# Two-layer image attention on one Trainium2 core: softmax sums from a column of ones in v, and layer-norm input transposed in one pass

## The chip, the cores and the metric

The kernel runs on one NeuronCore of a Trainium2 chip. Its time is the device time of one execution in microseconds (us); a result is the median of several executions. Five engines work side by side, each in the order of its own queue: TensorE (PE; its weight loads are shown as PEld), VectorE (DVE), ScalarE (ACT), GpSimd (POOL) and SyncE (SP). They wait for one another by semaphores. DMA queues move data between memories.

## The reference

The input `x` is 4 images of 32x32 positions with 768 channels, float32. Two layers follow, each `x = x + attention(groupnorm(x))`, with 12 heads of 64 channels over all 1024 positions of an image.

```
layer 0: q, k, v = heads(x @ Wq + bq), ...           # no norm on q, k, v
layer 1: q, k, v = layer_norm(dwconv3x3(heads(x @ w_qkv.T + b_qkv)))   # over the 64 channels of a head
attn = softmax(q @ k.T / 8 + rel_h(q)[:, :, :, :, None] + rel_w(q)[:, :, :, None, :])
o    = attn @ v            (layer 1: + q)
out  = o @ Wp + bp
```

`layer_norm` subtracts the mean over the 64 channels of a head and divides by the standard deviation; then it multiplies by `g` and adds `b`, each of 64 values. Before `g` and `b` the 64 channels of a normed vector therefore sum to zero. `rel_h` and `rel_w` are products of q with tables of relative positions.

## The kernel before, in words

**Tiling.** Work goes in pairs of heads, since two heads of 64 channels fill the 128 partitions. There are 8 stages (image, layer), in the order (0,0), (1,0), (0,1), (1,1), (2,0), (3,0), (2,1), (3,1), and 6 pairs in each: 48 pairs, 24 of each layer. Attention of a pair (`attend`) has two chunks of 512 queries. A chunk has two groups of four key tiles of 128. For a group TensorE makes four score tiles `s` (128 keys x 2 heads x 512 queries), ACT takes their exponential into `e` (L760), and later TensorE multiplies `v` with them into `av` (L775). The softmax's denominator comes from DVE: it adds all eight `e` tiles of a chunk into `acc` (L767 once, L769 six times), and TensorE sums `acc` over the keys with a matrix of ones into `z` (L717). ACT and DVE make the inverse from `z` (L724 to L733), and DVE multiplies it onto `weighed`, a copy of `av` (L710).

**Order.** The order on TensorE, DVE, ACT and POOL is written out by hand. `attend` is a generator that stops 8 times in a chunk, so 16 steps in a pair. At each step a table `events` runs pieces of other work: the preparation of the next pair (`plan`: number of the step, piece), group norm of the next stage, projection of the stage before (`project`). What `copy(av)` leaves behind is worked off by `more()`: `sums`, `result` and `finish`, one each time that a group of scores or of `av` has been issued.

**Preparing a pair of layer 1.** For each of q, k and v: products with the weights (`padded`, tile `qkv` of L131), ACT puts them into a padded image (L520), DVE makes the 9 taps of the convolution (`taps`, L535 and L537), and then:

- `centre`: TensorE multiplies the convolved image, as the stationary operand, with a 128x128 matrix `CENTRE` (identity less the mean of each head). That transposes it, tokens on partitions, and takes the mean off at once. The two halves of columns are two matmuls (`halves`, L131). Tile `ln_c`; ACT writes its square into `squared` (L550) and itself into `c` (L551).
- `squares`: DVE sums `squared` over each head (L555). `norm`: ACT and DVE make the inverse root (L153 to L160), and DVE multiplies (L566), for v straight into the attention's operand `vt`.
- `back`: q and k are transposed back by TensorE (L573, tile `ln_t`), and ACT writes them (L488, L489, L497).
- `positions` and `split` make the position bias from q (tile `rel`, L595 to L612); POOL's queue spreads it by DMA into `bias` (L622).

**PSUM.** Of eight banks, two are for a score tile `a`, one for `av`, one is `small`; two places of two banks each (`place_b`, left, and `place_c`, right) hold in turn the second and third score tile of a group and single banks for other work. `bank()` hands the singles out in a fixed rotation, `behind_scores` (b, b, c, c) or `behind_av` (c, c, small, b, b). A score pair in a place waits until both singles there have been read.

**Shared memory.** `shared` is one large SBUF tile in parts: two `centred`, two padded images, two `convolved`, one `squared`.

The functions that the diff touches:

Of the kernel before, what the change touches and what calls it, by code (L numbers as in the profile page):

```python
# [9 lines left out]
F32 = mybir.dt.float32  # L10
F32R = mybir.dt.float32r
I32 = mybir.dt.int32
AF = mybir.ActivationFunctionType
# [21 lines left out]
NSMALL = 81  # L35


IDENT, GROUP, CENTRE, HEADS, ONES = 0, P, 2 * P, 3 * P, 3 * P + 2
NCONST = 3 * P + 2 + D


LIMIT = 1e15
# [3 lines left out]
def two_layers(ctx: ExitStack, tc: tile.TileContext, keep, x_in, wqkv, wproj, rels, windows, vrow, small, const, onehot, picks, out):  # L46
# [78 lines left out]
    def small_bank(name):  # L125
        return ps_small.tile([P, 512], F32, tag="small", name=name)

    def halves(ps, a, b, start=True, stop=True, **kw):

        for lo in (0, D):  # L130
            nc.tensor.matmul(ps[lo : lo + D], a[:, lo : lo + D], b, start=start, stop=stop, **kw)  # L131
# [15 lines left out]
    def col(c, lo=0, hi=P):  # L147
        return sm[lo:hi, c : c + 1]
# [50 lines left out]
    def in_turn(what, of):  # L199
        counts[what] += 1  # L200
        return of[counts[what] % 2]
# [166 lines left out]
    class Pair:  # L368
# [170 lines left out]
        def centre(self, s):  # L539

            y = self.y[s]
            self.c[s] = c = in_turn("c", centred)
            for h in range(2):
                cols = slice(h * HALF, (h + 1) * HALF)
                ps = bank("ln_c")
                first = h * (HALF + S)
                for t in range(NKT // 2):
                    tokens = slice(first + t * P, first + (t + 1) * P)
                    halves(ps[:, t * P : (t + 1) * P], y[:, tokens], cst[:, CENTRE : CENTRE + P])
                nc.scalar.activation(squared[:, cols], ps, AF.Square)  # L550
                nc.scalar.copy(c[:, cols], ps)  # L551

        def squares(self, s):
            self.v = v = stat.tile([P, 2 * NKT], F32, tag="lnv", name="lnv")
# [3 lines left out]
        def norm(self, s):  # L558
            r = rsqrt(self.v, 2 * NKT, "ln")
            c = self.c[s].rearrange("p (a d) -> p a d", d=D)  # L560
            dst = c
            if s == 2:

                self.make_vt()
                dst = self.vt.rearrange("p t (j d) -> p (t j) d", d=D)
            nc.vector.tensor_tensor(dst, c, r.unsqueeze(2).to_broadcast([P, 2 * NKT, D]), ALU.mult)  # L566

        def back(self, s, h):

# [55 lines left out]
        def plan(self):  # L625

            Q, K, V = 0, 1, 2
            if not self.layer and not in_sevens(self.i):
                return [
                    (0, lambda: self.plain(Q, 0)),  # L630
                    (2, lambda: self.plain(Q, 1)),
                    (4, lambda: self.plain(K, 0)),
                    (5, lambda: self.positions(0)),
                    (6, lambda: self.plain(K, 1)),
                    (7, lambda: self.positions(1)),
                    (8, lambda: self.split()),
                    (8, lambda: self.plain_v(0)),
                    (10, lambda: self.plain_v(1)),
                ]
            if not self.layer:  # L640
                pieces = [
                    (0, lambda: self.sevens(Q, False)),
                    (2, lambda: self.sevens(Q, True)),
                    (6, lambda: self.positions(0)),
                    (8, lambda: self.positions(1)),
                    (10, lambda: self.split()),
                ]
                if self.hp % 2 == 0:
                    pieces += [(8, lambda: self.sevens(V, False)), (10, lambda: self.sevens(V, True))]
                return [(r + shift(self.i), piece) for r, piece in pieces]  # L650

            pieces = [
                (-8, lambda: self.padded(Q, 0)),
                (-6, lambda: self.padded(Q, 1)),
                (-4, lambda: self.padded(K, 0)),
                (-2, lambda: self.padded(K, 1)),
                (2, lambda: self.padded(V, 0)),
                (4, lambda: self.padded(V, 1)),
                (3, lambda: self.centre(Q)),
                (5, lambda: self.squares(Q)),  # L660
                (7, lambda: self.norm(Q)),
                (8, lambda: self.centre(K)),
                (9, lambda: self.back(Q, 0)),
                (9, lambda: self.back(Q, 1)),
                (10, lambda: self.squares(K)),
                (10, lambda: self.positions(0)),
                (11, lambda: self.positions(1)),
                (12, lambda: self.norm(K)),
                (12, lambda: self.split()),
                (13, lambda: self.centre(V)),  # L670
                (14, lambda: self.back(K, 0)),
                (14, lambda: self.back(K, 1)),
                (14, lambda: self.squares(V)),
                (15, lambda: self.norm(V)),
            ]

            taps = (
                (Q, -4, (2, 2, 2, 2, 1)),
                (K, 2, (2, 2, 2, 2, 1)),
                (V, 8, (2, 2, 3, 2)),  # L680
            )
            for s, r, counts in taps:
                lo = 0
                for n in counts:
                    pieces.append((r, lambda s=s, lo=lo, n=n: self.taps(s, lo, lo + n)))
                    r, lo = r + 1, lo + n
            return pieces
# [4 lines left out]
    def attend(pair, os):  # L692
# [12 lines left out]
        for c in range(T // QC):  # L705
            cols = slice(c * QC, (c + 1) * QC)

            def copy(av):
                weighed = one.tile([P, QC], F32, tag="weighed", name="weighed")
                nc.scalar.copy(weighed, av)  # L710
                return weighed

            def sums(weighed, acc, c=c):

                z = small_bank("z")
                for j in range(2):
                    nc.tensor.matmul(  # L717
                        z[j * D : (j + 1) * D, :], cst[:, ONES : ONES + D], acc[:, j, :],
                        start=True, stop=True,
                    )  # L720
                at = 2 * (pair.i * (T // QC) + c)
                t = work.tile([P, QC], F32, tag="t", name="t", bufs=1)
                inv = work.tile([P, QC], F32, tag="inv", name="inv", bufs=1)
                nc.scalar.activation(t, z, AF.Copy, accum_out=seen[:, at : at + 1])  # L724

                nc.scalar.activation(inv, t, AF.Ln, bias=tiny)
                nc.scalar.activation(inv, inv, AF.Exp, scale=-1.0, accum_out=seen[:, at + 1 : at + 2])
                return weighed, t, inv
# [12 lines left out]

            def finish(inv, cols=cols):

                if not pair.layer:
                    nc.scalar.activation(q[:, cols], inv, AF.Identity, bias=col(pair.column(2)))

            for g in range(0, NKT, 4):
                es = []
# [14 lines left out]
                more()  # L763
                if g == 0:
                    av = ps_av.tile([P, QC], F32, tag="av", name="av")
                    acc = work.tile([P, 2, QC], F32, tag="acc", name="acc", bufs=1)
                    nc.vector.tensor_tensor(acc, es[0], es[1], ALU.add)  # L767
                for e in es[2 * (g == 0) :]:
                    nc.vector.tensor_tensor(acc, acc, e, ALU.add)  # L769
                yield  # L770
                yield
                for t, e in enumerate(es):
# [6 lines left out]
                other_work(behind_av)  # L779
                more()  # L780
                if g + 4 == NKT:
                    rest.extend((sums, result, finish))
                    found = (copy(av), acc)
                yield
                yield

# [148 lines left out]
    for k, stage in enumerate(stages):  # L935
        call, sums, products = project(stage, oss[k])
        first = (k + 1) * NC * n_steps
        if k + 1 == len(stages):
            at(first - 12, call)
            for r, *what in ((-12, range(5), (0,)), (-10, range(5), (1,)), (-6, (0,), (2,))):  # L940
                at(first + r, lambda sums=sums, what=what: sums(*what))
            continue
        at(first + 2, call)
        late = stages[k + 1][1]
        for r, what in ((1, (0,)), (6, (1,)), (8, (2,)), (9, (3,)), (10, (4,))) if late else ((4, (0, 1)), (5, (2,)), (6, (3, 4))):
            at(first + r, lambda sums=sums, what=what: sums(what))

        for r, n in zip((9, 11, 13, 15, 17, 19) if late else (7, 9, 11, 13, 14, 15), (2, 1) * 3):
            for _ in range(n):
                at(first + r, lambda products=products: next(products))  # L950
# [259 lines left out]
def _laid_out(inp):  # L1210
# [24 lines left out]
    const[:, CENTRE : CENTRE + P] = eye - head  # L1235
    const[:, HEADS : HEADS + 2] = np.kron(np.eye(2), np.full((D, 1), 1.0 / D))
    const[:, ONES : ONES + D] = 1.0
    key = np.arange(T)
    onehot = np.concatenate([np.arange(S)[:, None] == key // S, np.arange(S)[:, None] == key % S])

# [36 lines left out]
```

## Time and profile before

| | |
|---|---|
| median of 3 runs | 3901.6 us (3901.35 to 3903.21) |
| the profiled execution | 3898.63 us, its span 3896.8 us |
| mean granted TensorE clock | 0.996 |
| TensorE busy | 3826.2 us (98% of the span) |
| DVE busy | 2674.1 us (69%) |
| ACT busy | 1849.1 us (47%) |
| POOL busy | 412.1 us (11%) |

The page of the profile lists busy time by engine, the span in 40 slices with busy tenths in each, DMA queues, the chain of work that ended last, and groups of instructions. A group's line has: line of the kernel, engine, operation, written and read tiles, shapes, number of instructions; then busy time in us and the mean duration in ns; then the idle time of the engine before them and what ended it. A float32 matmul is two instructions in these counts. Matmuls overlap, so the mean of one is longer than what it adds; the distance from one group's start to the next is what it costs. In a list of waits each line has who waited, for what, the sum in us, how often, and the longest.

### The profile page before, as it was taken

Reading aid. Unit: us, or ns where it says so; the run is one execution under the profiler, and the core shown is the slowest. Engines: PE = TensorE matmul, PEld = TensorE weight load, DVE = VectorE, ACT = ScalarE, POOL = GpSimd, SP = SyncE. Lnnn points to the kernel's source line nnn. Section 1 sums busy time; section 2 is a strip of 40 time slices with the busy share of each in tenths; the row PEclk is TensorE's granted clock in tenths of the full one; section 3 lists DMA queues with packets and bytes.
Section 4 is the critical chain, followed back from the end, with each engine's and each line's share of the span. In section 5 each row is a group of like instructions: output and inputs, shape, how many; then the busy total and the mean of one; then the engine's idle time right before and its main releaser. Section 6 shows DMA issues by size and latency. Waiting matters only on the chain.

```text
span 3896.8 us, 79900 instructions
## 1 busy us (share of the span) xinstructions
PE 3826.2 (98%) x34748; PEld 1720.1 (44%) x34748; DVE 2674.1 (69%) x3088; ACT 1849.1 (47%) x2741; POOL 412.1 (11%) x776
## 2 busy tenths in 40 slices
PE   8999999999999999999899999999999999999998
PEld 3535535544344443444445445355443444434442
DVE  2566454558789987799653554454686898878885
ACT  2455434445255553456434554254553555525562
POOL 0111000110000110000010010011100010000010
PEclk9999999999999999999999999999999999999999
DMA  4344452321421213311144132522124121142123
GB/s 148 105 118 124 124 165 61 106 71 39 119 90 35 51 49 94 115 35 39 44 133 124 51 79 60 176 59 72 43 56 153 35 58 42 39 119 58 35 48 95
DMA packets 184710, 318.11 MB, mean 82 GB/s; under 512 B 24352, under 2 KB 77472, under 8 KB 184352
## 3 DMA queue, kind: packets, MB, share of 16 engines
q1 hardware_dynamic: 122912, 212.19, 17.3%
q0 software_dynamic: 61440, 100.71, 11.3%
q8 instruction: 277, 4.54, 0.5%
q14 instruction: 81, 0.66, 0.1%
HBM read 172.23 MB, written 39.91 MB: 54 GB/s over the span
## 4 chain that ended last, share of the span: by engine, by line
PE 86%; DVE 11%; issue 1%; DMA 1%; ACT 1%; SPq 0%; POOL 0%; DVEq 0%
PE qkv L131 18%; PE s L753 15%; PE av L775 15%; PE m1m L131 4%; PE m3m L131 4%; PE m4m L131 4%; PE s L755 4%; DVE shared L537 3%; PE p3p L131 3%; DVE acc L769 3%; PE p1p L131 3%; PE p4p L131 3%; PE ln_c L131 3%; PE rel L595 3%; PE z L717 2%; PE m L131 2%
## 5 line engine op out<-in xcount | busy, mean ns | idle before, releaser
L760 ACT ACTIVATE e<-s 128x1024 f32<-128x1024 f32 x768 | 776.7, 1024 | 406.2 <-PE s L755 372.8
L769 DVE TENSOR_TENSOR acc<-acc,e 128x1024 f32<-128x1024 f32 x576 | 705.6, 1225 | 182.1 <-ACT e L760 130.4
L753 PE MATMUL s<-q,k 64*128 64x512 f32 x3072 | 816.5, 608 | 4.7 <-ACT e L760 3.8
L131 PE MATMUL qkv<-xn,wqkv_t 128*64 128x512 f32 x3648 | 813.4, 595 | 4.1 <-DVE gmean L324 4.1
L537 DVE SCALAR_TENSOR_TENSOR shared<-shared,sm 128x1056 f32<-128x1056 f32 x576 | 758.6, 1317 | 15.0
L755 PE MATMUL s<-bias,ones 64*128 64x512 f32 x1536 | 615.5, 794 | 4.7 <-DMA bias<-whole 2.5
L775 PE MATMUL av<-e,vt 128*64 128x512 f32 x2624 | 593.9, 594 | 0.0
L622 POOL DMA_DIRECT2D bias<-high x384 | 204.1, 551 | 3225.9 <-ACT high L611 2988.5
L131 PEld LDWEIGHTS qkv<-xn,wqkv_t 128*64 128x64 f32 x3648 | 253.7, 137 | 487.2 <-issue 480.5
L520 ACT ACTIVATE shared<-qkv,sm 128x512 f32<-128x512 f32 (+1 forms) x288 | 129.1, 501 | 633.0 <-PE qkv L131 633.0
L753 PEld LDWEIGHTS s<-q,k 64*128 64x128 f32 x3072 | 283.8, 188 | 260.8 <-issue 214.9
L775 PEld LDWEIGHTS av<-e,vt 128*64 128x64 f32 x2624 | 184.3, 137 | 347.0 <-issue 321.9
L767 DVE TENSOR_TENSOR acc<-e 128x1024 f32<-128x1024 f32 x96 | 117.5, 1224 | 274.0 <-ACT e L760 265.4
L755 PEld LDWEIGHTS s<-bias,ones 64*128 64x128 f32 x1536 | 150.2, 188 | 193.1 <-issue 188.0
L622 POOL DMA_DIRECT2D bias<-whole x384 | 206.9, 567 | 104.3 <-DVE whole L612 96.4
L710 ACT COPY weighed<-av 128x512 f32<-128x512 f32 x96 | 56.3, 586 | 268.8 <-PE av L775 268.8
L131 PEld LDWEIGHTS ln_c<-cst,shared 128*64 128x64 f32 x2304 | 130.4, 137 | 47.5 <-issue 36.0
L595 PEld LDWEIGHTS rel<-q,rel 64*32 64x32 f32 x6144 | 111.9, 106 | 80.7 <-issue 60.6
L131 PE MATMUL ln_c<-cst,shared 128*64 128x128 f32 x2304 | 138.3, 273 | 5.5 <-ACT high L611 2.5
L131 PE MATMUL m4m<-xn,wqkv_t 128*64 128x512 f32 x528 | 122.3, 599 | 4.0 <-issue 3.0
L595 PE MATMUL rel<-q_t,rel 64*32 64x32 f32 x6144 | 123.6, 195 | 2.1 <-issue 2.1
L405 DVE TENSOR_TENSOR shared<-shared,m3m 128x512 f32<-128x512 f32 x66 | 45.4, 687 | 115.8 <-PE m3m L131 115.7
(151 smaller groups left out, 4223.5 us busy)
## 6 DMA issues: line engine op xcount, KB each, us to landing
bias<-high POOLq DMA_DIRECT2D x384, 128.0 KB, 2.8
bias<-whole POOLq DMA_DIRECT2D x384, 128.0 KB, 3.0
wqkv_t<-in_wqkv SPq DMA_DIRECT2D x78, 384.0 KB, 3.1
wqkv_t<-mixed SPq DMA_DIRECT2D x66, 384.0 KB, 3.1
wproj_t<-mixed SPq DMA_DIRECT2D x48, 384.0 KB, 3.3
wqkv_t<-in_wqkv SPq DMA_DIRECT2D x66, 192.0 KB, 2.5
xn<-in_x SPq DMA_DIRECT2D x24, 512.0 KB, 8.4
x<-in_x SPq DMA_DIRECT2D x48, 256.0 KB, 3.3
```

Of the source, the lines that this page charges most:

```text
L131: nc.tensor.matmul(ps[lo : lo + D], a[:, lo : lo + D], b, start=start, stop=stop, **kw)
L520: nc.scalar.activation(self.pad[s][:, rows, there : there + src.shape[2]], src, AF.Identity, bias=col(self.column(s)))
L537: nc.vector.scalar_tensor_tensor(y, window, tap, y, ALU.mult, ALU.add)
L595: nc.tensor.matmul(ps[lo : lo + S, k * S : (k + 1) * S].rearrange("p (b c) -> p b c", b=2), rel[rows, 2 * self.layer + i, first : first + ...
L622: nc.gpsimd.dma_start(sets, some.unsqueeze(1).to_broadcast([D // 2, 2, QC]))
L717: nc.tensor.matmul(z[j * D : (j + 1) * D, :], cst[:, ONES : ONES + D], acc[:, j, :], start=True, stop=True,)
L753: nc.tensor.matmul(ps[:, j, :], k[rows, keys], q[rows, cols], start=True, stop=False)
L755: nc.tensor.matmul(ps[:, j, :], ones[rows, keys], bias[c][rows, kt // 2, :], start=False, stop=True,)
L760: nc.scalar.activation(e, ps, AF.Exp)
L767: nc.vector.tensor_tensor(acc, es[0], es[1], ALU.add)
L769: nc.vector.tensor_tensor(acc, acc, e, ALU.add)
L775: nc.tensor.matmul(av[j * D : (j + 1) * D, :], pair.vt[:, kt, j * D : (j + 1) * D], e[:, j, :], start=(kt == 0), stop=(kt == NKT - 1),)
```

## The change

**Layer 1's denominators.** The last channel of each head's `v` in `vt` is overwritten with ones after the norm (`memset` in `norm`). The last row of each head in `av` is then the sum of its exponentials. `copy` sends that row by two DMAs from ACT's queue to the 64 partitions of the head, tile `t`. `acc` and its adds stay only for layer 0. Since the normed `v` sums to zero over a head, its last channel's result is minus the sum of the others: `sums` multiplies `weighed` with a new 128x128 constant `WHOLE` (identity, last column -1, corner 0) in two halves, into the bank that `z` had, and ACT copies it back into `weighed`. A step `landed`, which issues nothing, is put before `sums`, so `sums` and `result` come one `more()` later each. Before the last stage's projection one piece moves from step -6 to -4.

**The norm's input.** `centre` only transposes (`nc.tensor.transpose` with the identity, one matmul per tile). DVE sums each head's 64 channels from PSUM, and a second DVE operation takes 1/64 of it off while it moves the tile to `c`. The square is one ACT instruction over all 1024 columns from `c`, a piece of its own (`square`), one or two steps later; `squares` moves one step back.

```
-                    halves(ps[:, t * P : (t + 1) * P], y[:, tokens], cst[:, CENTRE : CENTRE + P])
-                nc.scalar.activation(squared[:, cols], ps, AF.Square)
-                nc.scalar.copy(c[:, cols], ps)
+                    nc.tensor.transpose(ps[:, t * P : (t + 1) * P], y[:, tokens], ident)
+                of = sums[:, h * NKT : (h + 1) * NKT]
+                heads = ps.rearrange("p (a d) -> p a d", d=D)
+                nc.vector.tensor_reduce(of, heads, AX.X, ALU.add)
+                nc.vector.scalar_tensor_tensor(
+                    c[:, h * HALF : (h + 1) * HALF].rearrange("p (a d) -> p a d", d=D),
+                    of.unsqueeze(2).to_broadcast([P, NKT, D]), -1.0 / D, heads, ALU.mult, ALU.add,
+                )
+
+        def square(self, s):
+            nc.scalar.activation(squared, self.c[s], AF.Square)
...
             nc.vector.tensor_tensor(dst, c, r.unsqueeze(2).to_broadcast([P, 2 * NKT, D]), ALU.mult)
+            if s == 2:
+                nc.vector.memset(dst[:, :, D - 1 :], 1.0)
...
                 (3, lambda: self.centre(Q)),
-                (5, lambda: self.squares(Q)),
+                (4, lambda: self.square(Q)),
+                (6, lambda: self.squares(Q)),
...
-                (10, lambda: self.squares(K)),
+                (10, lambda: self.square(K)),
+                (11, lambda: self.squares(K)),
...
-                (14, lambda: self.squares(V)),
+                (14, lambda: self.square(V)),
+                (15, lambda: self.squares(V)),
...
             def copy(av):
+
                 weighed = one.tile([P, QC], F32, tag="weighed", name="weighed")
                 nc.scalar.copy(weighed, av)
-                return weighed
...
+                if not pair.layer:
+                    return weighed, acc
+                t = work.tile([P, QC], F32, tag="t", name="t", bufs=1)
+                for rows in heads:
+                    nc.scalar.dma_start(t[rows], weighed[rows.stop - 1 : rows.stop, :].unsqueeze(1).to_broadcast([1, D, QC]))
+                return weighed, t
...
+            def sums(weighed, of, c=c):
+
+                z = small_bank("z" if not pair.layer else "whole")
                 at = 2 * (pair.i * (T // QC) + c)
-                t = work.tile([P, QC], F32, tag="t", name="t", bufs=1)
                 inv = work.tile([P, QC], F32, tag="inv", name="inv", bufs=1)
-                nc.scalar.activation(t, z, AF.Copy, accum_out=seen[:, at : at + 1])
+                if pair.layer:
+                    t = of
+                    halves(z, cst[:, WHOLE : WHOLE + P], weighed)
+                    nc.scalar.copy(weighed, z)
+                    nc.scalar.activation(inv, t, AF.Copy, accum_out=seen[:, at : at + 1])
+                else:
+                    t = work.tile([P, QC], F32, tag="t", name="t", bufs=1)
+                    for j, rows in enumerate(heads):
+                        nc.tensor.matmul(z[rows, :], cst[:, ONES : ONES + D], of[:, j, :], start=True, stop=True)
+                    nc.scalar.activation(t, z, AF.Copy, accum_out=seen[:, at : at + 1])
...
                 if g == 0:
                     av = ps_av.tile([P, QC], F32, tag="av", name="av")
-                    acc = work.tile([P, 2, QC], F32, tag="acc", name="acc", bufs=1)
-                    nc.vector.tensor_tensor(acc, es[0], es[1], ALU.add)
-                for e in es[2 * (g == 0) :]:
-                    nc.vector.tensor_tensor(acc, acc, e, ALU.add)
+                if not pair.layer:
+                    if g == 0:
+                        acc = work.tile([P, 2, QC], F32, tag="acc", name="acc", bufs=1)
+                        nc.vector.tensor_tensor(acc, es[0], es[1], ALU.add)
+                    for e in es[2 * (g == 0) :]:
+                        nc.vector.tensor_tensor(acc, acc, e, ALU.add)
...
-                    rest.extend((sums, result, finish))
-                    found = (copy(av), acc)
+                    rest.extend((landed, sums, result) if pair.layer else (sums, result, finish))
+                    found = copy(av)
...
-            for r, *what in ((-12, range(5), (0,)), (-10, range(5), (1,)), (-6, (0,), (2,))):
+            for r, *what in ((-12, range(5), (0,)), (-10, range(5), (1,)), (-4, (0,), (2,))):
```

More of the change, by code (lines that the diff above doesn't have):

```diff
@@ L35 @@
 NSMALL = 81
-IDENT, GROUP, CENTRE, HEADS, ONES = 0, P, 2 * P, 3 * P, 3 * P + 2
-NCONST = 3 * P + 2 + D
+IDENT, GROUP, CENTRE, HEADS, ONES, WHOLE = 0, P, 2 * P, 3 * P, 3 * P + 2, 3 * P + 2 + D
+NCONST = 4 * P + 2 + D
 LIMIT = 1e15
@@ L542, in centre @@
             self.c[s] = c = in_turn("c", centred)
+            sums = stat.tile([P, 2 * NKT], F32, tag="mean", name="mean")
             for h in range(2):
-                cols = slice(h * HALF, (h + 1) * HALF)
                 ps = bank("ln_c")
@@ L710, in copy, with landed @@
                 nc.scalar.copy(weighed, av)
-                return weighed
[L713 to L720, printed above, removed]
+                if not pair.layer:
[4 more added lines that the diff above has]
+                return weighed, t
+            def landed(*found):
+                return found
+            def sums(weighed, of, c=c):
+                z = small_bank("z" if not pair.layer else "whole")
                 at = 2 * (pair.i * (T // QC) + c)
-                t = work.tile([P, QC], F32, tag="t", name="t", bufs=1)
                 inv = work.tile([P, QC], F32, tag="inv", name="inv", bufs=1)
-                nc.scalar.activation(t, z, AF.Copy, accum_out=seen[:, at : at + 1])
+                if pair.layer:
[8 more added lines that the diff above has]
+                    nc.scalar.activation(t, z, AF.Copy, accum_out=seen[:, at : at + 1])
                 nc.scalar.activation(inv, t, AF.Ln, bias=tiny)
@@ L742, in finish @@
             def finish(inv, cols=cols):
-                if not pair.layer:
-                    nc.scalar.activation(q[:, cols], inv, AF.Identity, bias=col(pair.column(2)))
+                nc.scalar.activation(q[:, cols], inv, AF.Identity, bias=col(pair.column(2)))
             for g in range(0, NKT, 4):
@@ L1237, in _laid_out @@
     const[:, ONES : ONES + D] = 1.0
+    whole = np.eye(D)
+    whole[:, -1] = -1.0
+    whole[-1, -1] = 0.0
+    const[:, WHOLE : WHOLE + P] = np.kron(np.eye(2), whole)
     key = np.arange(T)
```

## The prediction

> **What bounds the kernel now.** I read the page first: busy shares, slices, then the chain that ended last.
>
> ```profile
> PE 3826.2 (98%) x34748; PEld 1720.1 (44%) x34748; DVE 2674.1 (69%) x3088; ACT 1849.1 (47%) x2741; POOL 412.1 (11%) x776
> PE  8999999999999999999899999999999999999998
> DVE  2566454558789987799653554454686898878885
> PE 86%; DVE 11%; issue 1%; DMA 1%; ACT 1%; SPq 0%; POOL 0%; DVEq 0%
> ```
>
> TensorE has work in every slice. A busy row can still hide slack, so I laid its timeline end to end. A run of 24 qkv instructions always takes 5.15 to 5.30 us to the next group's start, an av run 3.43 to 3.58. Everything above the usual spacing adds up to 58 us in 3897. So a microsecond taken out of TensorE's stream is a microsecond of time, and other engines matter only where they make it wait. DVE is the candidate: 8 to 9 tenths in layer 1's slices.
>
> The list of waits, TensorE alone, shows how little that is today:
>
> ```profile
> PE p1p L131 <- DVE os_sums L850: 5.8, 4, 1.4
> PE s L753 <- ACT e L760: 3.8, 3, 1.5
> PE ln_t L573 <- DVE shared L566: 3.4, 2, 1.7
> PE z L717 <- DVE acc L769: 1.8, 1, 1.8
> ```
>
> So taking `acc` off DVE is worth little by itself. The other half touches TensorE: `ln_c`. First the groups, each shape by itself (busy, mean ns), then a stretch of TensorE's timeline (start, us):
>
> ```profile
> L131 PE MATMUL ln_c<-cst,shared 128*64 128x128 f32 x2304 | 138.3, 273 | 5.5 <-ACT high L611 2.5 <-DVE shared L537 2.3 <-DVE t_ln L157 0.7
> L573 PE MATMUL ln_t<-cst,shared 128*128 128x128 f32 x384 | 52.4, 279 | 3.4 <-DVE shared L566 3.4
> ...
> 1009.92 5.37 PE L131 MATMUL qkv<-xn,wqkv_t 128*64 128x512 f32 x24
> 1015.12 1.92 PE L131 MATMUL ln_c<-cst,shared 128*64 128x128 f32 x32
> 1016.87 2.74 PE L131 MATMUL p4p<-os_sums,wproj_t 128*64 128x512 f32 x12
> ...
> 1030.70 1.09 PE L573 MATMUL ln_t<-cst,shared 128*128 128x128 f32 x8
> 1031.72 5.37 PE L131 MATMUL qkv<-xn,wqkv_t 128*64 128x512 f32 x24
> ```
>
> A `centre` call has 8 tiles of 128x128. Today it issues 32 instructions (two column halves, two passes each) and holds TensorE for 1016.87 - 1015.12 = 1.75 us. Two `back` calls transpose 8 tiles of the same size with 8 instructions, 1.02 us. The new `centre` is the second form.
>
> [...] a quarter of the instructions, 1.02 against 1.75 us; the time ratio is 1.7, and I use the time. [...] after holes the granted clock is 0.87 in the stretch 1846 to 1884 us. [...] The nearest row is L845, which reads 512 from PSUM in 0.75 us; I take that for the second operation[...].
>
> **Part by part.**
>
> (1) `centre` on TensorE. 72 calls (24 pairs, three parts), each 1.75 - 1.02 = 0.73 us shorter: 52.6. Followed by scores, ln_c took 1.85 (20 calls): 2.0 more. Entering full-width mode costs 0.10 (qkv to ln_c 5.15, qkv to ln_t 5.25): 7.2 back. **-47.4 us**, all on the path. If the entry costs nothing, -55; if leaving costs 0.10 too, -40.
>
> (2) `centre` off ACT, onto DVE. ACT loses 144 squares and 144 copies (0.60, 0.59) and gets 72 squares of 1024 from SBUF (about 1.05, L611): -97 us. [...] What matters is when the bank comes free: ACT finished 3.15 us after ln_c's start. An idle DVE would finish half one at about 0.8 + 1.45 = 2.25, half two at 3.7. A DVE behind its queue is later, and scores, `back` and products wait for these banks.
>
> (3) Layer 1 without `acc`. 48 chunks lose 7 adds of 1.22: DVE -411. The memset of ones is 24 times about 0.1. DVE's balance is -206 us.
>
> (4) z stays two halves of the same shape (0.91), and moves from after the scores to after av: no change in TensorE time. ACT gets a copy of z (0.59, 48 times) and issues 96 DMAs. None is issued by ACT now; SP's take 0.32 to 0.49 each, so some +35 us, against the 97 freed. Per chunk two issues put 0.7 us ahead of the next exps; the first exp has about 1 us before the third `a`-bank score needs it. Bounds: 0, and 0.5 us a chunk (24) if an issue takes twice that. I take 0. Landing: 128 KB pieces of bias land in 2.8 to 3.0 us; from copy to use lie a scores group and an av, 4.55 + 3.43. Hidden, with 5 us to spare; SP and POOL are not passed.
>
> (5) `result` two steps later, squares one step later. `weighed` is free again before the next av copy (DVE may be some 13 us late). Nothing on the path except at the end, below.
>
> **Where DVE's new duty meets TensorE**, by replaying the queues with the rows' durations. In a usual layer-1 pair:
> - Q's first half sits in the bank pair that the third score needs, 3.3 us after ln_c's start; DVE has caught up by then (no acc, result later), so 2.25: slack 1.
> - K's banks are needed after qkv, about 6.8 us: slack 3.
> - V's second half is needed by `back(K)` after av, at 4.5. Ahead of it DVE has K's norm, the split and two taps: they start when r_ln is there (acc no longer delays them) and end 5.15 us later, some 1.4 us after ln_c's start. Then 2.8: just in time, slack 0.3. I take 0.1 for each of 20: +2.
> - The projection piece three steps into a pair (4 times): two taps and 2.8 us of `centre` go before the L850 add that TensorE waits for; 6.95 us after ln_c's start against 6.1, so 0.85 each: +3.4.
> - Group norm's `gmean` behind V's centre (3 times): +1.8.
>
> Where layer 1 is prepared while layer 0 still runs (2 pairs), acc stays: DVE had some 77 us of work in 79 and gets 8.4 more. Q's squares then come 4 us later, ACT's exps queue behind them (1.8 us), V's banks come late (1.7): +3.8 each, **+7.6**; from 0 to 20.
>
> The two pairs before layer 0 or the end, with no qkv to fill in, are where holes are today:
>
> ```profile
> core 0: us, PE busy (x) PEld busy (x) DVE busy (x) ACT busy (x) POOL busy (x), PEclk, DMA share, GB/s
> ...
> 1846.00:1884.00 38.00, 29.21 (x394) 14.53 (x392) 29.32 (x35) 22.05 (x32) 8.30 (x16) 0.87 0.26 57
> 3757.00:3797.00 40.00, 31.80 (x434) 17.33 (x432) 31.43 (x38) 26.63 (x39) 8.30 (x16) 0.87 0.23 54
> ```
>
> There the chain is DVE: taps, four adds, K's norm, `whole`, then the bias DMA. Without the adds `whole` comes some 6 us earlier, of which 1.5 is already counted in (1): -4.3 each, **-8.6**; from 0 to -14. What is late next is ACT, which must do z's chain (2.9) and the square (1.0) before it empties rel's banks: 2.6 us of waiting stay.
>
> The tail: acc's wait before z goes (1.95), but z now follows the first products, and ACT's chain with one more copy starts later: the x22 products start 13.0 us after av instead of 11.7: +1.3.
>
> Sum: -47.4 - 8.6 + 2 + 3.4 + 1.8 + 7.6 + 1.3 = **-39.9**. The profiled execution took 3898.6 (span 3896.8), 3.0 below the median of the three runs, so: 3858.7 there, **3861** as a median.
>
> **The rivals.**
>
> A, DVE is never late: only (1) and the holes, and the usual DVE-made waits shrink too: -47 to -56, 3846 to 3854. For it: DVE has 206 us less to do. Against: where it is late is decided in two or three places. Chance 0.20.
>
> B, half is given back: V's slack of 0.3 is wrong by one tap (1.31) in 20 pairs, 20 us, or ACT's DMA issues delay exps by 0.5 a chunk: 3880 to 3890. Chance 0.17.
>
> C, slower: DVE becomes the bound through bank release. If it reaches every `centre` one step's two taps (2.62) later than I found, the slacks of 1, 3 and 0.3 give waits of 1.6, 0 and 2.3 a pair, 3.9 x 24 = 94: 3955. It decides from a mean extra wait of 0.67 us per `centre` ((40 + 8)/72) on. For it: DVE ran 90% in 1100 to 1180 us (72.14 of 80) and runs strictly in order; holes cost clock besides. Against: acc's removal takes more per pair (17.1) than `centre` adds (8.4). Chance 0.08.
>
> D, the edit doesn't do what it says: transposes of convolved tiles take as many passes as before. Then (1) is gone and the rest nearly cancels (+7.5 of net waits): 3898 to 3909. Against: L573 has the same tiles, operands and one instruction per tile. Chance 0.03.
>
> My own case, 3855 to 3872: 0.52.
>
> **How the numbers follow.** What a measurement can tell from no change is about 0.2%, 7.8 us. Faster: A, B and mine, less a little of B's upper tail: 0.88. Within: 0.04, D and some of B. Slower: 0.08, C. The range 3846 to 3889 holds A, mine and most of B, and takes in (1)'s bounds.
>
> **What would show it.** ln_c: 576 instructions, about 79 us busy, a call 1.0 to 1.1 us. DVE about 2470 busy, ACT about 1780, L769/L767 half as many. The waits list: TensorE waiting for DVE at ln_t or s for under 15 us in total. Wrong if ln_c keeps more than one instruction a tile, or if waits on DVE's new PSUM reads exceed 40 us.

## The result, and the profile after

| | before | after |
|---|---|---|
| median, 6 runs each | 3900.95 us (3899.05 to 3903.21) | 3887.19 us (3881.36 to 3891.82) |
| ratio | | 0.9964, 95% interval 0.9951 to 0.9976 |
| profiled execution, span | 3898.63, 3896.8 | 3891.82, 3890.0 |
| mean granted TensorE clock | 0.996 | 0.992 |

The change makes the kernel faster by 13.8 us, where 40 were forecast. The first lines of the page (busy time, two rows of slices, shares of the chain that ended last), now of after:

```profile
PE 3789.1 (97%) x33020; PEld 1647.4 (42%) x33020; DVE 2462.2 (63%) x3064; ACT 1786.4 (46%) x2573; POOL 412.1 (11%) x776
PE   8999999999999999999899999999999999999987
DVE  2566454559678877788254554454686887867773
PE 86%; DVE 8%; ACT 2%; DMA 2%; issue 1%; ACTq 0%; POOL 0%; SPq 0%; DVEq 0%
```

TensorE has 37 us less to do, but only 97% of the span is filled, and the last two slices dropped from 9 and 8 tenths to 8 and 7. DMA's share of the chain went from 1% to 2%, and ACT's too; these shares are rounded, and 1% of this span is 39 us. The group of instructions of the new `centre` is what it was meant to be:

```profile
L549 PE MATMUL ln_c<-cst,shared 128*128 128x128 f32 x576 | 78.6, 280 | 0.5 <-ACT e L786 0.5
```

So is a call in TensorE's timeline:

```profile
1011.43 5.37 PE L131 MATMUL qkv<-xn,wqkv_t 128*64 128x512 f32 x24
1016.74 1.09 PE L549 MATMUL ln_c<-cst,shared 128*128 128x128 f32 x8
1017.76 2.79 PE L131 MATMUL p4p<-os_sums,wproj_t 128*64 128x512 f32 x12
```

A quarter of the instructions, 1017.76 - 1016.74 = 1.02 us a call instead of 1.75, and the qkv group before it 0.1 longer. So the gain on TensorE is there. Where it went is in the list of waits of TensorE (who waited, for what: sum, times, longest):

```profile
PE s L781 <- DMA bias<-whole: 21.4, 4, 8.6
...
PE p3p L131 <- DVE os_sums L859: 8.4, 1, 8.4
PE p1p L131 <- DVE os_sums L878: 7.4, 8, 1.6
...
PE ln_t L584 <- DVE shared L553: 3.0, 5, 0.9
PE qkv L131 <- DVE gmean L324: 2.6, 3, 0.9
```

The same waits for pieces of the bias in before:

```profile
PE s L755 <- DMA bias<-whole: 2.5, 2, 1.5
PE s L755 <- DMA bias<-high: 2.2, 1, 2.2
```

The products p3p did not wait for this line of DVE's (L831 in before). The waits for DVE's new reads of PSUM (`ln_t`) are small. The new transfer is `t<-weighed`. This is the view of DMAs in after (KB each, median us from issue to landing) with the queues above it:

```profile
q1 hardware_dynamic: 122912, 212.26, 17.4%
...
q10 hardware_dynamic: 7680, 12.59, 5.9%
...
bias<-whole POOLq DMA_DIRECT2D x384, 128.0 KB, 3.0
...
t<-weighed ACTq DMA_DIRECT2D x96, 128.0 KB, 7.8
```

The columns of a queue are packets, MB and the share of the 16 engines' time. Queue 10 is ACT's and carries only t: 12.6 MB take 5.9%, where queue 1 moves 212 MB in 17.4%. Per byte, t's transfers hold the DMA engines 5.7 times as long, and the same 128 KB land in 7.8 us instead of 3.0.

What a slow transfer does to its neighbours shows in the pair that has no projection to fill it. Timeline of after, ACT's and POOL's DMA issues and TensorE's wait:

```profile
1847.40 1.12 ACTq L730 DMA_DIRECT2D t<-weighed  x2
1848.58 1.04 POOL L633 DMA_DIRECT2D bias<-high  x2 [2.73 <-issue]
1849.60 2.10 POOL L633 DMA_DIRECT2D bias<-whole  x4
...
1859.17 0.79 PE L781 MATMUL s<-bias,ones 64*128 64x512 f32 x2 [8.64 <-DMA bias<-whole]
```

t goes out at 1847.4, pieces of the bias from another queue 1 to 2 us behind it. The scores that need them stand until 1859. In the trace's packet records no packet of the bias's queue starts from 1847.6 to 1852.9, and in each us from 1849 to 1852 only 14 or 15 packets start, all of t, which last 1.08 to 1.09 us at the median. How the one queue holds up the other these records do not show. At the end of the kernel it is t itself that is late:

```profile
3808.63 1.26 ACTq L730 DMA_DIRECT2D t<-weighed  x2
...
3817.51 0.58 ACT L745 COPY weighed<-whole 128x512 f32<-128x512 f32 x1 [6.33 <-DMA t<-weighed]
...
3824.04 1.97 PE L131 MATMUL p3p<-os_sums,wproj_t 128*64 128x512 f32 x4 [8.35 <-DVE os_sums L859]
```

ACT may not overwrite `weighed` before the transfer has read it; the inverse, `result` and the projection's product follow. So the tail waits for the transfer itself. After this wait TensorE is slow for a while: 4 instructions of p3p took 1.97 us, and 8 took 1.89 before the wait. The granted clock was 1.00 from 3810 to 3818 us and 0.50 from 3818.4 to 3832.0, which is from within the wait on.

For before and after, and further below for four of the experiments, I laid TensorE's timeline end to end as in the prediction, and added up what each group takes above its usual spacing (us, from one profiled execution each; a row moves by up to 4 us with what is counted as usual). An unfilled pair is one that has no qkv or projection products to fill its waits; the tail is the end of the kernel:

| where | before | after |
|---|---|---|
| first unfilled pair (1830 to 1900) | 17.1 | 14.9 |
| the layer-0 pair behind it (1900 to 2000) | 1.1 | 12.1 |
| second unfilled pair, and the tail (from 3720) | 13.6 | 28.7 |
| everywhere else | 26.0 | 40.2 |
| sum | 57.8 | 96.0 |

What lies above the usual spacing grew by 38 us. Part of it is not waiting but work at a lower clock after the waits: the mean granted clock went from 0.996 to 0.992, and 0.004 of 3890 us is 16 us at most. The two profiled spans differ by 6.8, so some 45 us of TensorE's own work are gone. (The profiled execution of after lies 4.6 above its median.)

### The profile page after: what moved, and what is told of

Same layout as the page of the kernel before. It is cut to its first block, busy times and chain, and to the rows that moved or that the text cites. A ratio compares the mean times of both kernels' runs of the same rounds, so it can differ in the third digit from the quotient of the medians.

```text
span 3890.0 us, 76143 instructions
## 1 busy us (share of the span) xinstructions
PE 3789.1 (97%) x33020; PEld 1647.4 (42%) x33020; DVE 2462.2 (63%) x3064; ACT 1786.4 (46%) x2573; POOL 412.1 (11%) x776
## 3 DMA queue, kind: packets, MB, share of 16 engines
q1 hardware_dynamic: 122912, 212.26, 17.4%
## 4 chain that ended last, share of the span: by engine, by line
PE 86%; DVE 8%; ACT 2%; DMA 2%; issue 1%; ACTq 0%; POOL 0%; SPq 0%; DVEq 0%
PE qkv L131 18%; PE s L779 16%; PE av L803 15%; PE m4m L131 4%; PE m3m L131 4%; PE m1m L131 4%; PE s L781 4%; PE p3p L131 3%; PE rel L606 3%; PE p4p L131 3%; PE p1p L131 2%; PE m L131 2%; DVE shared L537 2%; PE ln_c L549 1%; PE z L750 1%
## 5 line engine op out<-in xcount | busy, mean ns | idle before, releaser
L786 ACT ACTIVATE e<-s 128x1024 f32<-128x1024 f32 x768 | 767.0, 1023 | 437.3 <-PE s L781 412.0
L781 PE MATMUL s<-bias,ones 64*128 64x512 f32 x1536 | 617.3, 797 | 21.4 <-DMA bias<-whole 21.4
L797 DVE TENSOR_TENSOR acc<-acc,e 128x1024 f32<-128x1024 f32 x288 | 352.8, 1225 | 113.4 <-ACT e L786 88.2
L795 DVE TENSOR_TENSOR acc<-e 128x1024 f32<-128x1024 f32 x48 | 58.8, 1225 | 225.0 <-ACT e L786 214.8
L552 DVE TENSOR_REDUCE mean<-ln_c 128x8 f32<-128x512 f32 x144 | 98.6, 685 | 111.5 <-PE ln_c L549 111.5
L563 DVE TENSOR_REDUCE lnv<-shared 128x16 f32<-128x1024 f32 x72 | 87.6, 1216 | 77.9 <-ACT shared L559 77.9
L606 PE MATMUL rel<-q,rel 64*32 64x32 f32 x6144 | 122.7, 195 | 4.0 <-issue 4.0
```

The costliest lines, as they stand in the source:

```text
L552: nc.vector.tensor_reduce(of, heads, AX.X, ALU.add)
L563: nc.vector.tensor_reduce(v, squared.rearrange("p (a d) -> p a d", d=D), AX.X, ALU.add)
L606: nc.tensor.matmul(ps[lo : lo + S, k * S : (k + 1) * S].rearrange("p (b c) -> p b c", b=2), rel[rows, 2 * self.layer + i, first : first + ...
L781: nc.tensor.matmul(ps[:, j, :], ones[rows, keys], bias[c][rows, kt // 2, :], start=False, stop=True,)
L786: nc.scalar.activation(e, ps, AF.Exp)
```

## The experiments

Theory 1: t's transfer reads one partition 64 times; this is slow (6.3 us to landing at best), pieces of bias behind it come late (up to 10.9 us to landing), and at the tail it is late itself. Theory 2: DVE is late in emptying `ln_c`'s banks, the prediction's rivals B and C. Theory 3: the issue of the transfers holds ACT (0.47 us each, once 4.1), so exponentials come late. Each set of runs has its own runs of before, with medians from 3898.9 to 3901.0; ratios are to those. Differences between kernels below are of medians, partly across sets, and a few us of them can be scatter: after's own six runs lie 10 us apart.

**spread: the same transfers from 64 partitions**

```
-nc.scalar.dma_start(t[rows], weighed[rows.stop - 1 : rows.stop, :].unsqueeze(1).to_broadcast([1, D, QC]))
+nc.scalar.dma_start(t[rows], weighed[rows])
...
-nc.scalar.activation(inv, t, AF.Copy, ...)      # layer 1
+nc.scalar.activation(inv, t, AF.Square, ...)    # and the logarithm from inv
```

> After, but t is read from 64 partitions, each its own row, instead of 64 times from one partition; same 96 transfers of 128 KB, same issues on ACT's queue. What is left out: the real denominators (the square of the weighed row stands in for them), so the output is not the attention's. Theory 1 (many reads of one partition: 6.3 us to landing at best, and pieces of bias behind them 8 to 11 us late): t lands in under 4 us, bias pieces in 3, the waits for bias<-whole and p3p's 8.35 us wait at the tail go; 3855 to 3865 us. Theory 2 (the vector engine is late in emptying banks, which took the gain back): no change, 3883 to 3891. Theory 3 (the issue itself holds ACT, 0.47 us and up to 4.1): little change, 3878 to 3890, ACT's waits ahead of s stay.

Measured: 3860.41 us, ratio 0.9899 [0.9884, 0.9914]. The transfer is now cheap, and the waits for bias and for p3p shrink. The view of DMAs of spread:

```profile
q10 hardware_dynamic: 7680, 12.59, 1.4%
...
t<-weighed ACTq DMA_DIRECT2D x96, 128.0 KB, 2.4
```

and TensorE's list of waits:

```profile
PE s L781 <- DMA bias<-whole: 4.1, 3, 1.6
PE s L781 <- DMA bias<-high: 3.0, 1, 3.0
...
PE p3p L131 <- DVE os_sums L859: 2.7, 1, 2.7
```

Nothing but the source of the read changed on the transfer's side: same bytes, same number, same queue. That is worth 26.8 us (3887.2 - 3860.4). Theory 2 expected none of it. In this kernel each row is also copied to its own partition, but that alone is not what makes a read cheap: the pieces of the bias come from 32 partitions, go to others, and land in 3.0 us.

**nodma: no transfer**

```
-for rows in heads:
-    nc.scalar.dma_start(t[rows], ...)
+nc.gpsimd.memset(t, 1.0)
```

> After, with t filled with 1.0 by POOL in place of the 96 transfers. What is left out: the denominators. Theory 1 and theory 3 alike: everything that the transfer costs goes, 3850 to 3862 us; theory 1 expects no more than 3 us between this and the run with spread sources, theory 3 expects this 20 us or more below that one. Theory 2: 3883 to 3891.

Measured: 3852.13, ratio 0.9875 [0.986, 0.989]. TensorE's waits in nodma, the two of interest:

```profile
PE s L780 <- DMA bias<-whole: 7.0, 3, 3.6
...
PE p3p L131 <- DVE os_sums L858: 2.4, 1, 2.4
```

All of the transfer costs 35.1 us, of which 26.8 are the reads of one partition. The other 8.3 are more than the 3 that theory 1 allowed and far less than theory 3's 20; the intervals of spread and nodma just overlap. No run takes the 8.3 apart. The profiled spans differ by 4.9 of them (3857.5 and 3852.6), and the table of places below by 1.4. Another 1.7 show in the traces: in the kernels that issue one pair of transfers a chunk from ACT, the scores group ahead of a `centre` call takes 4.62 us instead of 4.55, 24 times.

**c_only: the centre change alone**

Before, with the new `centre`, `square` and the steps of `squares`; `acc` and the old `sums` stay in both layers.

> Before, with the change of centre, square and squares alone: transposes in one pass, means on DVE, squares by ACT from SBUF; the sums of e on DVE and the old denominators stay, so no t transfer. DVE is then busy for about 2870 us. Theory 1: TensorE gains its 47 to 50 us, of which the vector engine's lateness takes more than in after, since the sums of e are still queued on it: 3860 to 3875 us, no waits for bias of 8 us. Theory 2: the centre change itself is what fails to pay: 3885 us or above.

Measured: 4009.86, ratio 1.0283 [1.0269, 1.0297], slower by 111 us. Theory 1 expected nothing like it; it lies above theory 2's bound, so for this edit by itself theory 2 is right. A slice row and the chain on the page of c_only:

```profile
DVE  2566545469799997889653554454797999979985
...
PE 63%; DVE 31%; ACT 3%; issue 2%; DMA 1%; DVEq 0%; SPq 0%; POOL 0%; ACTq 0%
```

and TensorE's list of waits:

```profile
PE s L764 <- ACT e L771: 50.7, 20, 4.6
PE ln_t L581 <- DVE shared L553: 34.8, 21, 4.3
...
PE s L764 <- DVE shared L553: 14.7, 10, 2.1
PE ln_c L549 <- DVE shared L537: 13.9, 2, 8.7
```

DVE is at 9 in layer 1's slices and has 31% of the chain. The largest wait, for ACT's exponentials, is DVE's at one remove. This is what ACT waits for ahead of them, in before and then in c_only:

```profile
ACT ln_ln L153 <- DVE lnv L556: 8.5, 5, 2.9
...
ACT ln_ln L153 <- DVE lnv L564: 88.4, 28, 6.0
```

This is the mechanism of the prediction's rival C (DVE the bound through bank release), with ACT held by DVE beside it, here at work because the adds of e are still on DVE. With the holes the clock fell too: the mean granted clock is 0.985, where before has 0.996, and 0.011 of 4008 us is 44 us at most of the 111. The two halves of the change belong together: ones in v make the room that the new `centre` needs.

**v_only: the ones in v alone**

Before, with the memset of ones, t by transfer, `WHOLE`, `landed`, the moved projection piece and layer 1 without `acc`; the old two-pass `centre`.

> Before, with ones in layer 1's v's last channel, t by transfer from ACT's queue and the sums of e gone from layer 1, but the old two-pass centre, so the vector engine is busy for about 2250 us and has least to be late with. Theory 1: the transfer costs about 30 us with nothing against it: 3920 to 3935 us, with the waits for bias and at the tail. Theory 2: nothing is lost here, 3892 to 3902 us.

Measured: 3916.02, ratio 1.0045 [1.0032, 1.0059]. Slower, with the waits that theory 1 names, though DVE has only 2277 us to do (waits of v_only):

```profile
PE s L770 <- DMA bias<-high: 11.0, 2, 6.2
PE s L770 <- DMA bias<-whole: 10.5, 2, 9.4
PE p3p L131 <- DVE os_sums L848: 8.3, 1, 8.3
```

The size was smaller than expected (17 us, not 20 to 35), since this half also brings something; v_nodma, below, shows how much.

**late_free: no transfer in the last two pairs of layer 1**

```
+if pair.hp >= NC - 2:
+    nc.gpsimd.memset(t, 1.0)
+    return weighed, t
```

> After, but in each batch's last two pairs of layer 1 (8 of the 48 chunks) t is filled with 1.0 by POOL; the other 40 chunks keep their transfer. What is left out: the denominators of those two pairs. The traces put the loss at the four places that these 8 chunks touch (the two pairs without a projection to fill them, the pair behind the first, the tail). Theory 1 as read there: nearly all of the 35 us between after and the run without transfers comes back, 3852 to 3862 us. If the loss is spread evenly over the chunks, a sixth of it comes back: 3879 to 3885.

The count in this expectation is wrong: the condition holds in the last two pairs of each of 4 images, 16 of 48 chunks, and so "evenly spread" would have meant a third, about 3875 us. Measured: 3856.57, ratio 0.9887 [0.9871, 0.9902]. 30.6 of the 35.1 us come back with a third of the transfers gone. The other 32 chunks keep their slow transfers and lose 4.4 us (3856.6 - 3852.1), no more than the scatter of the two: where qkv and projection fill the pair, t has its two steps and the bias is ahead of its use.

**from_sp: issued by SP**

```
-nc.scalar.dma_start(t[rows], ...)
+nc.sync.dma_start(t[rows], ...)
```

> After, with t's transfers issued by SP in place of ACT; the 64 reads of one partition stay. Theory 1 (the reads): landing still 6.3 us and more, bias still late; only ACT's hold of 3.1 us at 1928 us goes, 3880 to 3888. Theory 3 (the issue on ACT): the loss goes, 3855 to 3868.

Measured: 3881.97, ratio 0.9952 [0.9938, 0.9966], which overlaps after's. t lands in 6.3 to 10.9 us as before, and the waits for bias stay (list of waits of from_sp):

```profile
PE s L781 <- DMA bias<-high: 16.3, 2, 9.9
PE s L781 <- DMA bias<-whole: 10.1, 2, 9.1
...
PE p3p L131 <- DVE os_sums L859: 8.3, 1, 8.3
```

Theory 3 falls as the main cause: moving the issues off ACT is worth 5.2 us (3887.2 - 3882.0), within the two intervals. The landing is as slow from SP's queue as from ACT's: 8.0 us at the median against 7.8.

**relay and relay_sp: one row to 8 partitions, then 8 to 56**

```
 def copy(av):
...                              # for each head's partitions, lo to hi
+    nc.scalar.dma_start(t[lo : lo + 8], weighed[hi - 1 : hi, :].unsqueeze(1).to_broadcast([1, 8, QC]))
...
+def landed(weighed, t):
...
+    nc.scalar.dma_start(t[lo + 8 : hi], t[lo : lo + 8].unsqueeze(1).to_broadcast([8, 7, QC]))   # relay_sp: nc.sync
```

> After, with t filled in two transfers, both from ACT's queue: the row to 8 partitions, and one step later those 8 to the other 56 (7 reads of each). Nothing is left out. Theory 1: each lands in 2.2 to 3.5 us, no piece of bias is 8 us late; close to the run with spread sources, 3858 to 3868 us, with ACT issuing 192 transfers instead of 96 (45 us more of issue, beside other work). Theory 3: twice the issues, slower than after, 3890 to 3905.

> As the run before, with the second transfer from SP's queue. Theory 1: 3855 to 3868 us, unless SP's loads are held behind its wait for the first transfer. Theory 3: as after, 3880 to 3890.

Measured: relay 3873.30, ratio 0.9933 [0.9919, 0.9946]; relay_sp 3876.22, 0.9939 [0.9926, 0.9953]. Faster than after and not by what theory 1 promised. In relay the bias waits fell to 6.5 us in all, but two transfers one after the other are late at the tail, and ACT now waits for them. ACT also issues twice as often: the scores group ahead of a `centre` call takes 4.87 us, where after has 4.62, which in 24 places is 6 us. TensorE's list of waits in relay, then ACT's:

```profile
PE p3p L131 <- DVE os_sums L862: 7.0, 1, 7.0
```

```profile
ACT inv L749 <- DMA t<-t: 21.0, 21, 3.3
...
ACT ln_ln L153 <- DMA t<-weighed: 19.0, 10, 2.7
```

In relay_sp, waits of 6.8 and 6.2 us for bias are back; why was not tried further.

**v_nodma: ones in v, old centre, no transfer**

v_only with the `memset` of nodma.

> Before, with ones in layer 1's v and the sums of e gone there, the old two-pass centre, and t filled with 1.0 by POOL. What is left out: layer 1's denominators. If the prediction's sum is right in its parts, this edit by itself is worth about nothing once the transfer is gone: 3896 to 3902 us, and the centre change is then worth the difference to the same kernel with the new centre (3852.1), 44 to 50 us. If relief of the vector engine is worth something of its own, 3885 to 3893.

Measured: 3883.40, ratio 0.9953 [0.9939, 0.9966]. The relief of DVE is worth 17.6 us of its own, more than either range allowed. (The first range was not the prediction's sum, which has -7.3 for this relief.) With nodma this splits the change in three (medians):

| | transfer of t | no transfer | price of the transfer |
|---|---|---|---|
| old `centre`, ones in v | 3916.0 | 3883.4 | 32.6 |
| new `centre`, ones in v | 3887.2 | 3852.1 | 35.1 |
| worth of the new `centre` | -28.8 | -31.3 | |

**late_pe, pe_den and last_pe: denominators by TensorE**

```
+def last(weighed, c=c):
+    z = small_bank("z")
+    for rows in heads:          # LAST: ones in the row of channel 63 of each head
+        nc.tensor.matmul(z[rows, :], cst[rows, LAST : LAST + D], weighed[rows], start=True, stop=True)
+    return (weighed, *inverse(z, c))
+def others(weighed, t, inv):    # WHOLE's two diagonal blocks, then the copy into weighed
-rest.extend((landed, sums, result) ...
+rest.extend((last, others, result) ...
```

`late_pe` has this in 16 chunks (the condition of late_free), `pe_den` in all 48, `last_pe` in the 8 of images 1 and 3.

> After, but in the 8 chunks of each batch's last two pairs of layer 1 the denominators come from TensorE: one more pair of matmuls that takes channel 63 of each head to 64 partitions, in a step of its own ahead of the other channels' pair; the other 40 chunks keep their transfer. Nothing is left out. Theory 1: the run with those 8 chunks filled with ones (3856.6 us) plus 8 x 0.91 us (the z group's spacing) = 3864 us, range 3859 to 3869, faster than before and after. If the 40 kept transfers cost anything, more.

> The same with TensorE's denominators in all 48 chunks, no transfer of t at all; nothing is left out. Theory 1: the run without transfers (3852.1) plus 48 x 0.91 = 3896 us, range 3890 to 3900; that would be the price from which the transfer is the better way where it has room.

> After, with TensorE's denominators in the last two pairs of layer 1 of images 1 and 3 alone: 8 of the 48 chunks. (The two runs late_free and late_pe changed 16, the last two pairs of every image; the number 8 in their expectations was a miscount.) Nothing is left out. Theory 1, with the loss in the places around these 8 chunks: late_pe's 3867.2 less the 8 pairs of matmuls that it had in images 0 and 2, where the traces show no loss: 8 x 0.91 = 7.3, so 3860 us, range 3856 to 3866. If the transfers of images 0 and 2 cost something too, 3866 to 3870.

Measured: late_pe 3867.19, ratio 0.9912 [0.9898, 0.9925]; pe_den 3904.47, 1.0009 [1.0003, 1.0016]; last_pe 3858.19, 0.9889 [0.9873, 0.9906]. With the right count late_pe's expectation would have been 3871. pe_den costs 52.3 us over nodma, 1.09 a chunk instead of 0.91. Its price is in the timeline of last_pe:

```profile
3785.82 1.07 PE L751 MATMUL z<-weighed,cst 64*64 64x512 f32 x4 [0.69 <-ACT weighed L725]
3786.83 2.80 PE L131 MATMUL p4p<-os_sums,wproj_t 128*64 128x512 f32 x12
...
3789.55 0.19 PEld L758 LDWEIGHTS whole<-weighed,cst 64*64 64x64 f32 x4 [0.81 <-ACT inv L745]
3789.55 1.08 PE L758 MATMUL whole<-weighed,cst 64*64 64x512 f32 x4
3790.56 1.94 PE L131 MATMUL p3p<-os_sums,wproj_t 128*64 128x512 f32 x8
```

A pair of 64x64 tiles takes 1.01 us to the next group, and there are two of them for one group of 0.91: 2 x 1.01 - 0.91 = 1.11. **last_pe is the version that beats both kernels**: 29 us below after, 41 below before, and within 2 us of what was expected. It keeps 40 slow transfers and replaces the 8 that stood on the path. Less the price of those 8, 3858.2 - 8 x 1.11 = 3849.3, it is not above nodma's 3852.1, so the 40 show no cost. They are no faster for it: 45 pieces of the bias still land more than 6 us after their issue, as 60 do in after and none in spread, but the waits for bias are down to 6.9 us.

The places, for the kernels that decide (us above the usual spacing):

| where | v_nodma | nodma | spread | after | last_pe |
|---|---|---|---|---|---|
| first unfilled pair | 8.6 | 10.3 | 9.7 | 14.9 | 8.1 |
| layer-0 pair behind it | 5.0 | 2.6 | 4.7 | 12.1 | 3.1 |
| second unfilled pair, tail | 8.8 | 13.7 | 14.5 | 28.7 | 14.6 |
| everywhere else | 16.6 | 35.2 | 34.3 | 40.2 | 35.0 |

## Why the prediction was right in part and wrong in its sum

**Step (1), right.** 72 calls went from 128.1 to 73.4 us: -54.7, forecast 52.6 + 2.0. The qkv group ahead of a call takes 0.10 longer (46 times), 4.6 in all; the forecast charged this entry to all 72, 7.2. Net -50.1 against -47.4. The scores group ahead of the other calls took 0.07 longer in after (24 times), but this is not the entry: it is gone in nodma and from_sp, which have the same `centre` and issue no transfer from ACT. It belongs to step (4).

**Steps (2) and (3), right.** DVE 2462 us busy against 2470, ACT 1786 against 1780. The reduce took 0.685 us and the second operation 0.688, together 1.37. The forecast's +203 us for DVE was 144 times 1.41, an estimate of which 0.75 (L845 in before) was measured and the rest, the reduce, was not.

**Where DVE meets TensorE, right in size, less so in its parts.** Forecast +14.8 outside the unfilled pairs; between v_nodma and nodma, which differ only in `centre` and the steps that belong to it, the row "everywhere else" grows by 18.6. `ln_t` waits 3.0 us in all, five times (forecast 2 for V's second half, in 20 small pieces). The waits of p1p grew by 1.1 us, from 6.3 to 7.4 (forecast 3.4), and the largest growth is in the waits for ACT's exponentials, from 0.8 to 7.7. So it is partly luck that the sum fits. The new `centre` as a whole was put at -47.4 + 2 + 3.4 + 1.8 + 7.6 = -32.6 and measured -31.3.

**The unfilled pairs, mis-sized.** Forecast -8.6 for both and +1.3 at the tail, -7.3 for the relief of DVE. v_nodma gives -17.6. By the places it is 8.5 in the first unfilled pair, 4.8 in the second with the tail and 9.4 elsewhere, with 3.9 given back in the layer-0 pair behind the first. Most of the 9.4 lies in usual waits, which the sum took as unchanged and only rival A let shrink: those for DVE's `gmean` (4.1 us) are gone, and those for exponentials fell from 3.8 to 0.8. This error went the other way and hid 10 us of the next one.

**Step (4), wrong, and it decides.** It said: "Landing: 128 KB pieces of bias land in 2.8 to 3.0 us; from copy to use lie a scores group and an av, 4.55 + 3.43. Hidden, with 5 us to spare; SP and POOL are not passed." Three things failed in it.
- The nearest row was wrong. Pieces of bias have as many bytes but are read from 32 partitions; t is read from one. The landing is 6.3 to 10.9 us. The bounds that the step gave (0 to 24) were for ACT's issues, which did turn out small (5.2 us between after and from_sp); the landing had none.
- The distance of 4.55 + 3.43 holds in a filled pair. At the tail the products stand directly behind, and waited 8.4 us, where nodma has 2.4.
- POOL's queue is not passed, but its pieces of bias come late behind t. A transfer that is itself hidden made another late: 21.4 us of waits for `bias<-whole`, against 7.0 in nodma.

The term that was taken as 0 measured 32.6 to 35.1. The three terms of the sum were -32.6, -7.3 and 0; the runs, taken one after the other from before over v_nodma and nodma to after, give -31.3, -17.6 and +35.1, which is -13.8.

**The rivals.** B gave the right time, 3880 to 3890, for reasons that did not carry it: V's slack mostly held (`ln_t` waited five times, 3.0 us in all), and from_sp shows that ACT's issues are a small part at most. C did not happen in the change and did, with 111 us, in c_only. Of A, the shrinking of usual waits was true.

## What to carry to other kernels

Price a transfer by what it reads and not by its bytes alone: here a row that is broadcast from one partition landed in 7.8 us, and the same 128 KB read from 64 partitions in 2.4. Ask where in the kernel its use is nearest and which other transfers are issued right behind it, for that is where a hidden transfer costs; here 8 of 48 chunks paid nearly all. When two edits come together, try each alone: here either alone was a loss, the one because it needed the room that the other makes, the other because of its slow transfer.

## What the runs showed of the hardware that I had not expected

- **Packets that read one partition took longer than those that read 64.** In the trace's packet records, a 2 KB packet of t took 0.084 us at its fastest in after and 1.07 us or more in a quarter of the cases, with up to 16 packets in flight together. By the mean number in flight, the median in after is 0.10 us for a packet alone, 0.28 with 5, 0.57 with 9 and 1.08 with 15, though it does not rise at every step (0.27 with 12); in spread it is 0.10, 0.10, 0.10 and 0.16. Over all cases in spread it is 0.084 to 0.17 us (5th to 95th percentile). Summed over the 2 KB packets: 3651 us of engine time in after, 823 in spread. With 15 in flight that is one packet in about 0.07 us, an estimate from 1.08/15. That it takes one partition alone is not shown: in relay, where the larger transfer reads eight neighbouring partitions 7 times each, the median is still 0.31 us with 7 in flight (0.10 in spread, 0.47 in after). No run separates the one partition from its neighbours.
- **The DMA issues were not of one length.** On ACT in after one took 0.47 us at the median, but 2.5 to 4.1 us in four of 96; on SP in from_sp 0.56, and up to 4.1; in spread none was over 1.44. What the long ones waited for stays open.
- **Two 64x64 tiles were no cheaper than two of 128x64**: 1.01 us to the next group in last_pe (3785.82 to 3786.83) against 0.91 for z in before (1050.96 to 1051.87), each for 512 columns and ahead of p4p, so half the rows saved nothing here.
